# Layer 0 of a four-layer network: attention's first inputs and the mixer's last norm change their stage

## The chip, the cores and the metric

The kernel runs on one core of one Trainium2 chip. A core has a matrix engine (TensorE, PE in the profile; PEld is its weight load), a vector engine (VectorE, DVE), a scalar engine for activations (ScalarE, ACT), a general engine (GpSimd, POOL) and a sync engine that issues DMAs (SyncE, SP). SBUF is the memory the engines work in, 128 partitions wide; PSUM holds what PE produces. The metric is the device time of one execution in microseconds, lower is better.

## What is computed

Input x has the shape (4, 32, 128, 128): batch, time, node, feature. Four layers follow one another; the change touches the first, the three others stay. Layer 0 adds to x, after a group norm over features, the result of an attention over nodes followed by a selective state-space mixer over time:

```python
def _gat(h, adj, Wq, Wk, Wv, Wo, bo):
    q = (h @ Wq).reshape(BT, N, HEADS, HD)      # likewise k, v
    scores = einsum('bnhd,bmhd->bhnm', q, k) / sqrt(HD)
    scores = where(adj == 0, -1e9, scores)
    o = einsum('bhnm,bmhd->bnhd', softmax(scores), v)
    return h + o.reshape(BT, N, D_MODEL) @ Wo + bo

def _mamba(xt, ...):                            # x and z from in_proj, short convolution, silu
    dt = softplus(...); dA = exp(dt[..., None] * A); dBx = (dt * xc)[..., None] * Bm
    def step(hprev, inp):
        hnew = dA_t * hprev + dBx_t
        return hnew, einsum('bds,bs->bd', hnew, C_t)
    ...                                         # 32 steps, 16 states, 256 channels
    return ((ys + Dp * xc) * silu(z)) @ out_w + out_b
```

A layer norm (gain ns_g, ns_b) follows the attention, another (nt_g, nt_b) the mixer together with its own input.

## The kernel before, in words

x lies whole in SBUF as X, nodes on the partitions. `layer0` (L265) loads weights and then goes through the four batches, one after the other: `gat` (L379) is the attention of one batch, `mamba` (L671) its mixer. Each has pools of its own that are opened before and closed after it: l0g in SBUF and l0sc, l0po, l0px in PSUM for attention, l0m, l0m2 in SBUF and l0pa, l0y in PSUM for the mixer. The pools of one stage lie where those of the other lay, so that a tile's first writer waits for the last user of whatever was at its place. l0s (with the state S), l0w and the two PSUM banks pm are open through the whole layer.

**Attention** takes 8 groups of 4 time steps. First, once for a batch, `diags` (L401 to L408) makes three small columns and two diagonal matrices from the group norm's values gd, PE spreads them over the partitions (L412), and ACT copies the result to grow (L416). For a group g: four transposes of X on PE, the normed hg on DVE (L435), q and k on PE (L441) and ACT (L444), v on PE (L450) and DVE (L453), base on POOL (L457, two instructions; it needs grow and X), the scores on PE (L464 masks, L472 products), minima on DVE (L481), exponentials on ACT (L486), sums and reciprocals on DVE (L493, L494), the scaling on POOL (L498), transposes, copies (L506), the products with v (L513), the output projection (L526), residual, norm and the store into h1 (L558). hg, base and xn lie in S, which is free in that stage.

**The mixer** makes 32 steps. In each, four quarters (four states each) run through POOL (L702, the product of dt and A), ACT (L708, exponential), DVE (L722, times the state S) and DVE again (L730, four instructions, or L742 after ACT's L738), and PE reads the state (L755). Every 4 steps there is a block: its preparation (`mamba_block`) and its output, which is projected on PE (L823 to L829), copied by ACT (L835), and normed and added to X: statistics on DVE (L842, L844, L845), a power on POOL (L848), a shift on DVE (L852), the norm on ACT (L857), three instructions on POOL (L861, L862, L864). `gat_head` (L322) computes the group norm's values of the next batch inside the mixer after step 23: transposes, statistics, two small products with g4 (L356) with DVE work between them (L360 to L363), a power on POOL (L369).

**The order** is written by a planner, `Parts`. Every piece of work is a part with an engine, a cost in us, what it comes after, what it takes and frees (`hold`: how many buffers of a name there are), and a rank. `emit` repeatedly picks the earliest startable part by these costs and, within 0.15 us of it on the same engine, the lowest rank; a rank is step times pace plus an offset by kind (GAT_RANKS, PREP_RANKS, RANKS). `in_order` then fixes the order on each of PE, ACT, DVE and POOL for the whole plan. Each attention and each mixer is a plan of its own, so on every engine all of a mixer's instructions stand before all of the next attention's. The head's rank is T * pace with T = 32 and a pace of 25.5.

Of the kernel before, what the change touches and what calls it, by code (L numbers as in the profile page):

```python
# [187 lines left out]
class Kernel:  # L188
# [76 lines left out]
    def layer0(self):  # L265

        with self.pool("l0h", 1) as hp, self.pool("l0c", 1) as c:
            h1 = hp.tile([P, 3 + T, N], F32, tag="h1", name="h1")
            self.nc.gpsimd.memset(h1[:, :3, :], 0.0)


            with self.pool("l0s", 1) as m, self.pool("l0w", 2) as w, self.pool("l0pm", 2, True) as pm:
                S = m.tile([P, T * N], F32, tag="S", name="S")

                for t in range(0, T, 8):
                    self.load_x(0, t, t + 8)
                gw = self.gat_weights(c)
                with self.pool("l0k", 1) as k:
                    mw, built = self.mamba_weights(c, k)
                    for b in range(1, B):  # L280
                        self.load_x(b)
                    plan = Parts()
                    d = self.gat_head(plan, 0, gw, m, pm)
                    with self.in_order():
                        plan.emit()
                    built()
                for b in range(B):
                    with self.pool("l0g", 2) as g, self.pool("l0sc", 2, True) as ps, self.pool("l0po", 1, True) as po:
                        with self.pool("l0px", 1, True) as px:
                            blks = self.gat(b, h1, S, d, gw, mw, g, m, w, ps, po, px, pm)  # L290
                    with self.pool("l0m", 1) as y, self.pool("l0m2", 2) as v:
                        with self.pool("l0pa", 2, True) as pa, self.pool("l0y", 1, True) as py:
                            d = self.mamba(b, h1, S, blks, gw, mw, m, w, y, v, pa, py, pm)

    def gat_weights(self, c):
# [16 lines left out]
        att=-560, back=1038.5, base=200, den=-2290.5, diag=1387, eT=-3745, expo=1373, hg=-1936.5, norm=-205,  # L312
        o=-720.5, power=2945, proj=-444.5, q=-340.5, qo=-606, r=-2536, sc=-4037, scale=6881.5, smin=435,
        stats=4037.5, store=1820, turn=-662, v=3273.5, vo=-1137, x=401,
# [3 lines left out]
        back=-674.5, bc=5118, bct=1491.5, conv=1508, dabs=-687.5, dbc=1712, dexp=648.5, dln=-965, dplus=1619,  # L318
        dsub=2247.5, dtproj=441.5, one=-448.5, relu=-2119, umul=-703, xproj=836.5, xsilu=645, xturn=-1090.5,
    )  # L320

    def gat_head(self, plan, b, gw, c, pm, after=()):  # L322
# [53 lines left out]
        add(POOL, 0.6, power, [p])  # L376
        return d

    def gat(self, b, h1, S, d, gw, mw, w, m, w2, ps, po, px, pm):  # L379
# [3 lines left out]
        isq = 1.0 / math.sqrt(32)  # L383
        plan = Parts(window=250, patience=0.15)
        hold, pace, s = plan.hold, 144.5, {}
# [15 lines left out]
        def diags():  # L401
            c = s["c"] = w.tile([P, 2], F32, tag="gc", name="gc")
            nc.vector.tensor_tensor(c[:, 0:1], d[0][:, 2:3], d[0][:, 2:3], ALU.add)
            nc.vector.scalar_tensor_tensor(c[:, 1:2], d[0][:, 0:1], -1.0, c[:, 0:1], ALU.mult, ALU.mult)
            nc.vector.tensor_tensor(c[:, 1:2], c[:, 1:2], bo, ALU.add)
            s["D"] = w.tile([P, 2, P], F32, tag="gD", name="gD", bufs=1)
            for i in range(2):
                nc.vector.tensor_scalar(s["D"][:, i, :], self.ident, c[:, i : i + 1], None, ALU.mult)  # L408

        def spread():  # L410
            s["p"] = bank()
            nc.tensor.matmul(s["p"][:, :256], self.ones, s["D"].rearrange("p a b -> p (a b)"), start=True, stop=True)  # L412

        def rowed():
            s["row"] = w.tile([P, 2, P], F32, tag="grow", name="grow", bufs=1)
            nc.scalar.copy(s["row"].rearrange("p a b -> p (a b)"), s.pop("p")[:, :256])  # L416

        p = add("diag", 0, DVE, 1.2, diags)
        hp = hold("pm", 2)
        p = add("diag", 0, PE, 0.5, spread, [p], [hp])  # L420
        row = add("diag", 0, ACT, 0.4, rowed, [p], (), [hp])

        def group(g):
            v = {}
            for i, n in enumerate(("hg", "base", "xn")):
                o = 512 * (2 * i + g % 2)
                v[n] = S[:, o : o + 512]
            xs = X[:, b * T + 4 * g : b * T + 4 * g + 4, :]

            def inputs():  # L430
                v["x"] = bank()
                self.transposes(four(v["x"]), [xs[:, i, :] for i in range(4)])

            def scaled():
                nc.vector.tensor_scalar(  # L435
                    v["hg"], v.pop("x"), d[0][:, 0:1], d[0][:, 2:3], ALU.subtract, ALU.mult
                )

            def proj(n):
                v["p" + n] = bank()  # L440
                nc.tensor.matmul(v["p" + n], Wq if n == "q" else Wk, v["hg"], start=True, stop=True)  # L441

            def proj_out(n):
                nc.scalar.mul(new(v, n), v.pop("p" + n), -isq if n == "q" else 1.0)  # L444

            def values():
                v["pv"] = bank(px, "px")
                for i in range(4):
                    cs = slice(i * P, (i + 1) * P)
                    nc.tensor.matmul(v["pv"][:, cs], v["hg"][:, cs], Wv, start=True, stop=True)  # L450

            def values_out():
                nc.vector.tensor_copy(new(v, "v"), v.pop("pv"))  # L453
# [108 lines left out]
            h = {n: hold(n, 2) for n in ("q", "k", "v", "mn", "xn", "hg", "base")} | {n: hold(n, 1) for n in ("o", "r")}  # L562
            hx, hs, ho = hold("px", 1), [hold("ps", 2), hold("ps", 2)], hold("po", 1)
            hp = hold("pm", 2)
            p = add("x", g, PE, 0.5, inputs, (), [h["hg"], hp])
            x = add("hg", g, DVE, 0.6, scaled, [p], (), [hp])
            outs = []
            for n in ("q", "k"):
                hp = hold("pm", 2)
                p = add("q", g, PE, 0.95, lambda n=n: proj(n), [x], [h[n], hp], [h["hg"]])  # L570
                outs.append(add("qo", g, ACT, 0.55, lambda n=n: proj_out(n), [p], (), [hp]))
            pv = add("v", g, PE, 1.0, values, [x], [h["v"], hx], [h["hg"]])
            vo = add("vo", g, DVE, 0.6, values_out, [pv], (), [hx])
# [41 lines left out]
    def mamba_weights(self, c, k):  # L615
# [20 lines left out]
        ob4 = c.tile([1, 4, P], F32, tag="ob4", name="ob4")  # L636
        for i in range(4):
            nc.sync.dma_start(ob4[:, i, :], ins["L0_conv_out_b"].rearrange("(o n) -> o n", o=1))
# [22 lines left out]
    HEAD = 5  # L661
# [9 lines left out]
    def mamba(self, b, h1, S, blks, gw, mw, m0, w0, m, w, pa, py, pm):  # L671
# [15 lines left out]
        S, d = S.rearrange("p (s d) -> p s d", s=16), None  # L687
# [129 lines left out]
        def output(k, g):  # L817
# [15 lines left out]
            def fetch():  # L833
                g["x"] = w.tile([P, 4, P], F32, tag="xn", name="xn")
                nc.scalar.copy(g["x"].rearrange("p a f -> p (a f)"), g.pop("p"))  # L835

            def stats():
                st = w.tile([P, 4, 6], F32, tag="mst", name="mst")
                g["mv"] = w.tile([P, 4, 2], F32, tag="mmv", name="mmv")
                g["rs"] = w.tile([P, 4], F32, tag="mrs", name="mrs")  # L840
                for i in range(4):
                    nc.vector.bn_stats(st[:, i, :], g["x"][:, i, :])  # L842
                for i in range(4):
                    nc.vector.bn_aggr(g["mv"][:, i, :], st[:, i, :])  # L844
                nc.vector.tensor_scalar(g["rs"], g["mv"][:, :, 1], 1e-5, None, ALU.add)  # L845

            def power():
                nc.gpsimd.tensor_tensor(g["rs"], g["rs"], self.mhalf.to_broadcast([P, 4]), ALU.pow)  # L848

            def shift():  # L850
                g["nb"] = w.tile([P, 4], F32, tag="mnb", name="mnb")
                nc.vector.scalar_tensor_tensor(g["nb"], g["mv"][:, :, 0], -1.0, g["rs"], ALU.mult, ALU.mult)  # L852
# [16 lines left out]
            p = add("stats", 4 * k + 4, DVE, 2.0, stats, [p])  # L869
            p = add("power", 4 * k + 4, POOL, 1.0, power, [p])  # L870
            p = add("shift", 4 * k + 4, DVE, 0.2, shift, [p])
            p = add("norm", 4 * k + 4, ACT, 1.8, norm, [p])
            add("sums", 4 * k + 4, POOL, 4.3, sums, [p], free=[hx])


# [4 lines left out]
        for k in range(T // 4):  # L880
# [7 lines left out]
            if b + 1 < B and k == self.HEAD:  # L888
                plan.rank = T * pace
                d = self.gat_head(plan, b + 1, gw, m0, pm, [last["read", 0]])  # L890
        with self.in_order():
            plan.emit()
        return d
# [2257 lines left out]
```

## Time and profile before

| | us |
|---|---|
| median of 3 runs | 3819.91 (3813.42 to 3825.31) |
| the profiled execution | 3815.5 |
| its span in the trace | 3813.6 |
| layer 0 in it | 0 to about 2287 |

| engine | busy us | share of the span |
|---|---|---|
| PE | 3154.9 | 83% |
| DVE | 2963.4 | 78% |
| ACT | 2671.6 | 70% |
| POOL | 2482.6 | 65% |

The windows view gives the busy time of the engines in layer 0's stages:

| stage | us | PE | DVE | ACT | POOL |
|---|---|---|---|---|---|
| batch 0 attention, 32.0 to 160.0 | 128.0 | 111.3 | 86.1 | 87.8 | 70.8 |
| batch 0 mixer, 160.0 to 597.9 | 437.9 | 358.5 | 402.5 | 381.7 | 397.1 |
| batch 3 attention, 1727.7 to 1855.0 | 127.3 | 109.7 | 88.0 | 89.8 | 72.8 |
| batch 3 mixer, 1855.0 to 2287.0 | 432.0 | 362.9 | 392.1 | 379.9 | 394.6 |

A line of the timeline has start, duration, engine, line and operation, output and inputs, the number of instructions merged, and in brackets how long the engine had been idle before it and what ended that. Lines merged over several instructions overlap with lines between them. A group's line has engine, operation, tiles and count, the durations in ns (minimum, median, maximum), the first and last start in us, and the shape. In a wait, the first name is the instruction that waited, the second what it waited for.

### The profile page before, as it was taken

The page shows a single profiled execution, that of the slowest core. Times are in us where ns is not written, and L with a number is a line of the kernel's source. Part 1 is how long each engine was busy: PE and PEld are TensorE (multiplying, and loading weights), DVE is VectorE, ACT ScalarE, POOL GpSimd, SP SyncE. Part 2 cuts the span into 40 slices and gives each one's busy share as a digit, 9 for nine tenths or more (in the row PEclk, how much of TensorE's full clock was granted, in tenths as well). Part 3 has the DMA queues.
Part 4 walks back from the last instruction along what each step waited for, and adds up shares of the span by engine and source line. Part 5 has one row for each costly group of instructions (what it writes and reads, how often), then busy time and mean ns, then how long its engine had stood idle before and what let it go on. Part 6 is the DMA issues. An engine that isn't in the chain of part 4 may idle for free. (4 is left out here: it accounts for less than half of the span.)

```text
span 3813.6 us, 64481 instructions
## 1 busy us (share of the span) xinstructions
PE 3154.9 (83%) x23495; PEld 2067.5 (54%) x23495; DVE 2963.4 (78%) x7050; ACT 2671.6 (70%) x5577; POOL 2482.6 (65%) x1947
## 2 busy tenths in 40 slices
PE   6888877888878888877888878787868987988878
PEld 4545444555445554544555547665546753587655
DVE  5699996799996799996799975577869856386942
ACT  5899975899975899976899963334565654176753
POOL 3699985799985799975799970133456522067940
PEclk8898999899989899989899875797869998998989
DMA  3000000000000000000000000000002000700003
GB/s 127 1 1 1 1 1 1 1 1 1 1 1 1 1 1 1 1 1 1 1 1 1 1 7 12 1 1 1 1 9 90 1 1 1 269 5 1 1 1 89
DMA packets 51660, 61.38 MB, mean 16 GB/s; under 512 B 5853, under 2 KB 31146, under 8 KB 51210
## 3 DMA queue, kind: packets, MB, share of 16 engines
q1 hardware_dynamic: 36746, 42.12, 3.2%
q10 hardware_dynamic: 14592, 15.08, 1.1%
q8 instruction: 188, 3.08, 0.3%
q14 instruction: 134, 1.10, 0.1%
HBM read 48.80 MB, written 8.39 MB: 15 GB/s over the span
## 5 line engine op out<-in xcount | busy, mean ns | idle before, releaser
L702 POOL TENSOR_TENSOR e<-dt,Ar 128x1024 f32<-128x1024 f32 x496 | 1162.1, 2365 | 48.1 <-ACT pa L708 47.4
L722 DVE TENSOR_TENSOR pa<-pa,S 128x1024 f32<-128x1024 f32 x496 | 608.1, 1226 | 37.5 <-ACT pa L708 36.6
L730 DVE SCALAR_TENSOR_TENSOR S<-u,BC,pa 128x256 f32<-128x256 f32 x1488 | 615.3, 476 | 19.4
L708 ACT ACTIVATE pa<-e 128x1024 f32<-128x1024 f32 x496 | 503.2, 1018 | 82.0 <-DVE S L730 45.4
L755 PE MATMUL yp<-S,Dp 64*64 64x256 f32 x4096 | 350.8, 464 | 84.2 <-DVE S L730 46.0
L755 PE MATMUL yp<-S,D 64*64 64x256 f32 x4096 | 311.9, 412 | 55.8 <-DVE S L742 28.9
L755 PEld LDWEIGHTS yp<-S,Dp 64*64 64x64 f32 x4096 | 183.8, 160 | 232.1 <-issue 137.2
L755 PEld LDWEIGHTS yp<-S,D 64*64 64x64 f32 x4096 | 158.0, 140 | 190.7 <-ACT D L714 50.7
L714 ACT ACTIVATE D<-I,BC 128x64 f32<-128x64 f32 x1024 | 259.3, 336 | 2.7 <-PE yp L755 2.7
L944 PE MATMUL pm<-h,Wm 128*128 128x512 f32 x512 | 238.0, 605 | 1.0 <-ACT sz L910 1.0
L738 ACT ACTIVATE ub<-u,BC 128x256 f32<-128x256 f32 x496 | 210.8, 497 | 0.5 <-DVE S L742 0.3
L773 PE MATMUL pm<-I,y 128*128 128x64 f32 x1024 | 158.1, 281 | 50.5 <-ACT y L763 50.5
L498 POOL TENSOR_TENSOR e<-e,den 128x512 f32<-128x512 f32 x128 | 131.1, 1040 | 78.2 <-DVE den L494 36.6
L773 PEld LDWEIGHTS pm<-I,y 128*128 128x128 f32 x1024 | 147.9, 208 | 58.2 <-ACT y L763 58.2
L719 POOL TENSOR_TENSOR Dp<-I,BC 128x256 f32<-128x256 f32 x256 | 156.0, 621 | 31.0 <-PE yp L755 17.9
L742 DVE TENSOR_TENSOR S<-pa,ub 128x1024 f32<-128x1024 f32 x124 | 151.7, 1224 | 5.7
L944 PEld LDWEIGHTS pm<-h,Wm 128*128 128x128 f32 x512 | 91.3, 189 | 111.6 <-issue 98.3
L486 ACT ACTIVATE e<-sc,mn 128x128 f32<-128x128 f32 x512 | 145.5, 393 | 6.0 <-DVE mn L481 5.9
L763 ACT COPY y<-yp 128x512 f32<-128x512 f32 x128 | 73.6, 575 | 82.8 <-PE yp L755 82.8
L768 PE MATMUL pm<-xc,DD 128*128 128x128 f32 x512 | 127.6, 334 | 0.0
L481 DVE TENSOR_REDUCE mn<-sc 128x4 f32<-128x512 f32 x128 | 80.6, 682 | 49.2 <-PE sc L472 49.2
L768 PEld LDWEIGHTS pm<-xc,DD 128*128 128x128 f32 x512 | 84.9, 208 | 61.1 <-issue 53.6
(594 smaller groups left out, 8178.2 us busy)
## 6 DMA issues: line engine op xcount, KB each, us to landing
w<-in_L_ffn_weight_dram SPq DMA_DIRECT2D x22, 1024.0 KB, 14.2
w<-in_L_ffn_weight_dram ACTq DMA_DIRECT2D x10, 1024.0 KB, 13.2
out_dram<-o ACTq DMA_DIRECT2D x16, 256.0 KB, 2.9
out_dram<-o SPq DMA_DIRECT2D x16, 256.0 KB, 2.9
X<-in_x_dram SPq DMA_DIRECT2D x4, 512.0 KB, 4.8
A<-in_L_conv_A_log_dram SPq DMA_DIRECT2D x1, 2048.0 KB, 9.8
cw<-in_L_conv_conv_w_dram SPq DMA_DIRECT2D x1, 512.0 KB, 10.6
sh<-in_sh_dram SPq DMA_DIRECT2D x1, 512.0 KB, 3.9
```

Of the source, the lines that this page charges most:

```text
L702: nc.gpsimd.tensor_tensor(v["e", q], node("dt").unsqueeze(1).to_broadcast([P, 4, 256]), Ar[:, 4 * q : 4 * q + 4, :], ALU.mult)
L708: nc.scalar.activation(v["a", q], v.pop(("e", q)), AF.Exp, scale=-1.0)
L714: nc.scalar.activation(v["D", q][:, r, :], I2, AF.Copy, scale=g["BC"][:, i, s : s + 1])
L719: nc.gpsimd.tensor_tensor(v["D", q], I2.unsqueeze(1).to_broadcast([P, 4, 64]), C, ALU.mult)
L722: nc.vector.tensor_tensor(v["a", q], v["a", q], S[:, 4 * q : 4 * q + 4, :], ALU.mult)
L730: nc.vector.scalar_tensor_tensor(S[:, s, :], node("u"), Bt, a[:, r, :], ALU.mult, ALU.add)
L738: nc.scalar.activation(v["b", q][:, r, :], node("u"), AF.Copy, scale=g["BC"][:, i, s : s + 1])
L742: nc.vector.tensor_tensor(S4, v.pop(("a", q)), v.pop(("b", q)), ALU.add)
L755: nc.tensor.matmul(v["y"][o : o + 64, n, :256], D[ns, r, :], S[ns, s, :], start=(s < 2), stop=(s >= 14), skip_group_check=True,)
L768: nc.tensor.matmul(v["p"][:, j * P : (j + 1) * P], DD[:, j, :], g["xc"][:, j, cs], start=True, stop=False)
L773: nc.tensor.matmul(v["p"][:, o : o + 64], v["y"][:, n, j * P : (j + 1) * P], I2, start=False, stop=(n == 1))
L944: nc.tensor.matmul(g["x", j], Wm[:, i, j * P : (j + 1) * P], rows(4 * k + 3 - i), start=(i == 0), stop=(i == 3))
```

## The change

A new pool l0e, open through the layer and with two buffers of a name, holds attention's hg, q, k, v, gc and grow, and the mixer's xn with its small statistics tiles. hg leaves S; base and xn of attention move down in it. What were the first steps of attention become two methods, `gat_open` (the diagonals, their spread and copy; the diagonals lie in a buffer of hg) and `gat_inputs` (x, hg, q, k, v of one group). The mixer of batches 0 to 2 calls them for the next batch, for groups 0 and 1, after the head, in its own plan; there v goes through pm instead of px, and all these parts have the rank 31 * pace. The head's rank goes from 32 * pace to 27 * pace. The mixer's last block leaves its norm (`close`) to the next attention's plan; in the last batch it stays. In the norm of every block, the addition of 1e-5 and the shift go from DVE to POOL, which now has four small instructions in place of one. GAT_RANKS and PREP_RANKS have new values. In the first attention, which opens itself, the transposes come after grow. out_b is loaded by one DMA in place of four and read with a stride of 0. The descriptor scratch of the program is set to 1024.

```diff
-            with self.pool("l0s", 1) as m, self.pool("l0w", 2) as w, self.pool("l0pm", 2, True) as pm:
+            with (
+                self.pool("l0s", 1) as m, self.pool("l0w", 2) as w, self.pool("l0e", 2) as e,
+                self.pool("l0pm", 2, True) as pm,
+            ):
...
-            d = self.mamba(b, h1, S, blks, gw, mw, m, w, y, v, pa, py, pm)
+            early = self.mamba(b, h1, S, blks, gw, mw, m, w, e, y, v, pa, py, pm)
...
+    def gat_open(self, add, hold, d, after, gw, e, pm):
...
+            c = s["c"] = e.tile([P, 2], F32, tag="gc", name="gc")
...
+            s["D"] = e.tile([P, 512], F32, tag="hg", name="hg")[:, :256].rearrange("p (a b) -> p a b", a=2)
...
+        p = add("diag", 0, DVE, 1.2, diags, after)
+        hp = hold("pm", 2)
+        p = add("diag", 0, PE, 0.5, spread, [p], [hp])
+        s["ready"] = add("diag", 0, ACT, 0.4, rowed, [p], (), [hp])
+        return s
+
+    def gat_inputs(self, add, hold, s, b, g, gw, e, pm, px):
...
+        hp = hold("pm", 2)
+        p = add("x", g, PE, 0.5, inputs, [s["ready"]], [h["hg"], hp])
+        x = add("hg", g, DVE, 0.6, scaled, [p], (), [hp])
+        v["outs"] = []
+        for n in ("q", "k"):
+            hp = hold("pm", 2)
+            p = add("q", g, PE, 0.95, lambda n=n: proj(n), [x], [h[n], hp], [h["hg"]])
+            v["outs"].append(add("qo", g, ACT, 0.55, lambda n=n: proj_out(n), [p], (), [hp]))
+        hx = hold("px", 1) if px else hold("pm", 2)
+        p = add("v", g, PE, 1.0, values, [x], [h["v"], hx], [h["hg"]])
+        v["vo"] = add("vo", g, DVE, 0.6, values_out, [p], (), [hx])
...
+        if early:
+            s = early
+            s["ready"] = None
+            s.pop("close")(lambda kind, at, *args, **kwargs: add("c" + kind, 0, *args, **kwargs))
...
+        else:
+            s = self.gat_open(add, hold, d, (), gw, ew, pm)
...
-            for i, n in enumerate(("hg", "base", "xn")):
+            if g not in s["v"]:
+                self.gat_inputs(add, hold, s, b, g, gw, ew, pm, px)
+            v = s["v"][g]
+            for i, n in enumerate(("base", "xn")):
...
-                nc.vector.tensor_scalar(g["rs"], g["mv"][:, :, 1], 1e-5, None, ALU.add)

             def power():
+                g["nb"] = e0.tile([P, 4], F32, tag="mnb", name="mnb")
+                nc.gpsimd.tensor_scalar(g["rs"], g["mv"][:, :, 1], 1e-5, None, ALU.add)
+                nc.gpsimd.tensor_scalar(g["nb"], g["mv"][:, :, 0], -1.0, None, ALU.mult)
                 nc.gpsimd.tensor_tensor(g["rs"], g["rs"], self.mhalf.to_broadcast([P, 4]), ALU.pow)
-
-            def shift():
-                g["nb"] = w.tile([P, 4], F32, tag="mnb", name="mnb")
-                nc.vector.scalar_tensor_tensor(g["nb"], g["mv"][:, :, 0], -1.0, g["rs"], ALU.mult, ALU.mult)
+                nc.gpsimd.tensor_tensor(g["nb"], g["nb"], g["rs"], ALU.mult)
...
+            if early and k == T // 4 - 1:
+                early["close"] = lambda add: close(add, None, [])
+            else:
+                close(add, p, [hx])
...
-                plan.rank = T * pace
-                d = self.gat_head(plan, b + 1, gw, m0, pm, [last["read", 0]])
+                plan.rank = self.HEADED * pace
+                d, p = self.gat_head(plan, b + 1, gw, m0, pm, [last["read", 0]])
+
+                def ahead(kind, at, *args, **kwargs):
+                    plan.rank = self.EARLIER * pace + at
+                    return plan.add(*args, **kwargs)
+
+                early = self.gat_open(ahead, hold, d, [p], gw, e0, pm)
+                for g in range(self.EARLY):
+                    self.gat_inputs(ahead, hold, early, b + 1, g, gw, e0, pm, None)
```

## The prediction

> **What bounds the kernel now.** I read the windows view first, cut at the stage boundaries of layer 0. Four times an attention stage is followed by a mixer stage, so the trace has three places where a mixer ends and the next attention begins. Each holds a hole some 25 us long. The columns are length, then busy us (instructions) of PE, PEld, DVE, ACT, POOL, the granted clock, DMA:
>
> ```profile
> 1711.50:1736.80 25.30, 15.19 (x105) 9.21 (x106) 5.64 (x29) 6.25 (x13) 9.61 (x8) 0.80 0.00 1
> 581.00:606.50 25.50, 14.66 (x100) 8.79 (x100) 6.42 (x29) 6.25 (x13) 9.61 (x8) 0.80 0.00 0
> 1147.70:1173.00 25.30, 14.56 (x92) 8.73 (x96) 6.23 (x29) 6.25 (x13) 9.62 (x8) 0.80 0.00 1
> ```
>
> DVE works about 6 of 25 us, ACT 6, POOL 10: the holes are waiting, not work. The timeline of the third shows the order:
>
> ```profile
> 1710.27 1.22 DVE L742 TENSOR_TENSOR S<-pa,ub 128x1024 f32<-128x1024 f32 x1
> ...
> 1718.27 0.39 PE L829 MATMUL pm<-ident,h 128*128 128x128 f32 x2
> ...
> 1726.46 1.26 POOL L864 TENSOR_TENSOR X<-X,xn 128x512 f32<-128x512 f32 x1
> 1727.75 0.16 DVE L403 TENSOR_TENSOR gc<-gd 128x1 f32<-128x1 f32 x1 [5.79 <-POOL X L864]
> ...
> 1728.61 1.52 DVE L435 TENSOR_SCALAR S<-pm,gd 128x512 f32<-128x512 f32 x2
> ...
> 1734.60 1.03 PE L464 MATMUL sc<-far,identb 128*128 128x512 bf16 x4
> 1735.55 0.98 PEld L472 LDWEIGHTS sc<-k,q 32*128 32x128 f32 x32 [0.42 <-issue]
> 1735.56 1.17 PE L472 MATMUL sc<-k,q 32*128 32x128 f32 x32
> ...
> 1736.76 2.48 DVE L481 TENSOR_REDUCE mn<-sc 128x4 f32<-128x512 f32 x4 [6.63 <-PE sc L472]
> ```
>
> The last scan step ends at 1711.49 (L742), the mixer's last projection on PE at 1718.66 (L829). The last norm then crosses ACT, DVE, POOL, ACT, POOL until 1727.72 (L864), and only then does attention's first DVE instruction start (L403): its small tile lies where the mixer's xn lay. After it come hg, q, k, and at 1736.76 the first softmax minimum. Attention thus starts 18.1 us after PE is done with the mixer.
>
> Inside the mixer DVE is the engine that is rarely idle: from 1655.0 to 1711.5 it is busy 53.45 of 56.50 us, against 43.53 for POOL and 38.76 for ACT. By line (ns are minimum/median/maximum), three lines that touch only SBUF vary widely there, and two that read PSUM do not:
>
> ```profile
> L845 DVE TENSOR_SCALAR mrs<-mmv x32: 170/2056/2201, 231.1 to 2279.3; 128x4 f32<-128x4 f32 x32
> L852 DVE SCALAR_TENSOR_TENSOR mnb<-mmv,mrs x32: 161/502/1715, 236.1 to 2280.6; 128x4 f32<-128x4 f32 x32
> L363 DVE TENSOR_TENSOR gd<-gd,gmv x4: 159/2193/2193, 17.2 to 1651.3; 128x1 f32<-128x1 f32 x4
> L435 DVE TENSOR_SCALAR S<-pm,gd x32: 781/803/810, 33.0 to 1804.1; 128x512 f32<-128x512 f32 x32
> L453 DVE COPY v<-px x32: 658/670/692, 43.2 to 1824.7; 128x512 f32<-128x512 f32 x32
> ```
>
> Four elements per partition take 0.17 us when POOL is idle and 2.06 in the median: they end when POOL's 2.36 us product (L702) ends.
>
> **The change, part by part.** The profiled execution took 3815.5 us (span 3813.6, 1.9 around it); it lies 4.4 under the median 3819.91. I sum against 3815.5.
>
> A. *Hole.* Groups 0 and 1 have hg, q, k and v in their own pool before the mixer ends, and attention's first buffers no longer wait for the last norm. What is late next is the projection on PE, since every plan keeps each engine in order: scores can start at 1718.7, and L464 to the end of L472 took 1734.60 to 1736.73, 2.13 us. First minimum at 1720.85 instead of 1736.76: 15.9 us. The norm's statistics, now first on DVE in attention, wait for ACT's copy at 1719.3 and take 1.4 us to 1720.7, still in time. 3 x -15.9 = **-47.7**.
>
> B. *Attention after the first minimum.* It loses two v groups on PE (1.05 + 1.16) and DVE (0.68 + 0.66), one diagonal product (0.4 PE, 0.4 ACT), and gains 1.24 DVE, 1.65 ACT and 1.8 + 3.9 POOL of the moved norm. POOL is busy 73 of 127 us there and hides its part. I take -1 each, **-3**; ends -5 (all of the PE and DVE work shortens it) and +4 (the norm's DVE and ACT work delay the first groups).
>
> C. *Early inputs in three mixers.* They become ready after POOL's power, near 1655 to 1668, where DVE has no slack, so DVE's time counts in full: hg 2 x 0.80, v 2 x 0.67 = 2.94, read from PSUM and so unmoved by POOL. The five small instructions of the diagonals take 1.04 beside an idle POOL (L403 0.16, L404 0.16, L405 0.16, L408 0.48 for two). Beside a busy one no row shows them; the nearest are L361 to L363, the same kind in the same place: 1.73, 0.16, 2.19. So 5, and 8 in all. Low end 4 (quiet rows). High end 20: each of the five waits out a 2.36 us product (11.8), and PE, whose diagonal product stands ahead of the scan's reads in its order, waits as it did for L363 (5.5). PE's 7 us and ACT's 2.8 us of this work stay beside DVE, as these were busy 41.66 and 38.76 of 56.5. 3 x 8 = **+24** (12 to 60).
>
> The Trainium skill, "SBUF — State Buffer", section "Who interferes with whom", speaks against this part: VectorE and GpSimd share a port pair as an exclusive lock, taken by tensor_scalar in its two-port modes and by anything with two SBUF inputs. By the rule all five may be held, an estimate of 12 us instead of 5, which would make C +44 and the time 3787; L362, 0.16 between two held ones, says that not every one is.
>
> D. *Norm off DVE.* L845 and L852 were 44.8 and 15.9 us of DVE over the mixers; both go, for three short POOL instructions that cost 0.79 more than L848 alone (start to start 1.78 at L541 to L544, against 0.99). DVE wins 2.4 per block of 4 steps, but POOL is idle only some 2.5 us of 55 there (53.2 busy of 56.0 between 886 and 942), and becomes the bound. The most is 2.5 - 0.8 = 1.7 per block; I take half, 0.9. With 6 such blocks in 4 mixers: **-22**. Ends: -41 (all of 1.7) and +25 (32 blocks, POOL the bound throughout).
>
> E. *First attention.* Its first DVE instruction waited 3.72 us for ACT's L654, whose tile lay under it; the new pool lies elsewhere, so it can follow Wm at 28.5 instead of 32.19. Against that the transposes now stand behind the diagonal product on PE (0.4 + 0.6) and hg behind them. Three DMA issues fewer on SP (0.3 each) bring the loads behind them 0.9 earlier. **-2** (-4 to +2).
>
> F. *New ranks* reorder attention and the mixer's first block; the head's rank falls from 32 to 27 steps. No row shows the new order. PE is busy 110 of 127 us in an attention, so the gain has an end: 17 each; for the loss I take the same size. Value **0**, the order that the trace has. The smaller descriptor scratch is used by no queue here (no DMA is issued by POOL): 0. The last mixer's tail: POOL's four instructions against POOL then DVE, +0.2: 0.
>
> Sum: -47.7 - 3 + 24 - 22 - 2 = -50.7, so 3764.8 by the profiled execution, 3769.2 by the median. I say **3767**.
>
> **Rivals.**
> 1. *Fuller gain.* The diagonals fall where POOL is idle (C = 12) and DVE's relief is used whole (D = -41): -47.7 - 3 + 12 - 41 - 2 = -82, 3736. For it: POOL waited 11.9 us for ACT's pa in one mixer (L702), which waits for DVE. Against it: POOL has little room.
> 2. *The hole moves into the mixer.* Early work at its dear end for three mixers, +45, and no net gain in D: -47.7 - 3 + 45 - 2 = -8, 3810. For it: DVE's 53.45 of 56.50. Against: only five instructions can be held.
> 3. *Slower: in-order queues behind held DVE work.* The planner prices the diagonals at 1.2 us; on the chip they could take 12. PE's spread, x, q and k are placed by the planner's time, ahead of the scan's reads, and whoever needs those reads (y copy, next step's sums on DVE) waits too. At 5.5 us (L356 behind L363) for each of spread and two groups, C is 3 x (14.7 + 16.5) = 94: -47.7 - 3 + 94 - 22 - 2 = +19, 3837. It decides from (47.7 + 3 + 22 + 2) / 3 = 25 us per mixer on.
> The change not doing what it says would show the first minimum still behind L864: within 5 of no change; it is counted with rival 2.
>
> **Numbers.** Forecast (3745 to 3797) 0.57; rival 1 (3715 to 3745) 0.20; rival 2 (3797 to 3831) 0.15; rival 3 0.08. About 0.3% (11.5 us) is what a measurement here can tell from no change. Faster by more: 0.57 + 0.20 + 0.08 of rival 2 (below 3808) = 0.85; same 0.07; slower 0.08. The range 3725 to 3812 leaves out a third of rival 1 (0.06), the upper part of rival 2 (0.06) and rival 3 (0.08).
>
> **What would show it.** A: the first L481 of attention 2 to 4 within 3 us of the last projection, no wait on L864. C: the early diagonals' mean duration in the mixer, and DVE's busy time after them. D: the pace of a middle block under 55 us, POOL's idle time gone. E: the first attention's first minimum before 40.77. I am wrong if scores wait for something that I don't see behind the projection, if the early instructions stall PE, or if the new ranks move an attention by more than 5 us.

## The result, and the profile after

The changed kernel takes 3863.84 us in the median of 4 runs (3858.76 to 3872.33), beside 3822.61 (3813.42 to 3826.67) for the kernel before: 1.0113 times as long, 95% interval 1.0087 to 1.014. I had said 3767, with 3725 to 3812 as the range and 0.08 for slower. Its profiled execution took 3864.56, with a span of 3862.7 and a mean granted clock of 0.867 (before 0.886).

The windows view of the changed kernel at the three boundaries, from the last scan step to the first minimum (columns as in the prediction):

```profile
1753.10:1763.60 10.50, 10.50 (x94) 8.02 (x95) 1.49 (x9) 1.17 (x2) 0.00 (x0) 0.84 0.01 2
602.30:611.30 9.00, 8.89 (x95) 6.80 (x96) 1.57 (x11) 1.17 (x2) 0.73 (x1) 1.00 0.01 2
1176.30:1185.40 9.10, 8.86 (x94) 6.77 (x95) 1.67 (x10) 1.17 (x2) 0.00 (x0) 1.00 0.01 2
```

The hole of 25 us is 9 to 10.5 long, and PE is busy throughout: the boundary is now work of PE. The timeline of the third:

```profile
1751.80 1.22 DVE L784 TENSOR_TENSOR S<-pa,ub 128x1024 f32<-128x1024 f32 x1
...
1754.52 1.49 PE L517 MATMUL sc<-far,identb 128*128 128x512 bf16 x3
...
1761.49 0.39 PE L871 MATMUL pm<-ident,h 128*128 128x128 f32 x2
...
1762.02 1.17 PE L525 MATMUL sc<-k,q 32*128 32x128 f32 x32
...
1762.53 0.87 DVE L884 BATCH_NORM_STATS2 mst<-xn 128x6 f32<-128x128 f32 x4 [4.12 <-ACT xn L877]
...
1763.60 0.66 DVE L534 TENSOR_REDUCE mn<-sc 128x4 f32<-128x512 f32 x1
```

Scores follow the last projection at once (L525 after L871) and the first minimum comes 1.7 us after it, where it was 18.1. Three of attention's four masks (L517) even run on PE before the mixer's end: that all of a mixer's instructions stand before all of the next attention's is so in the kernel before and no longer in the changed one.

Of the three DVE lines that varied beside POOL, the two of the norm are now POOL's (L890 to L893, the last one below), and five early diagonal instructions are new on DVE. The lines of the first three in the changed kernel (ns, minimum/median/maximum; of each four, one is the first attention's, beside an idle POOL, and takes 159):

```profile
L893 POOL TENSOR_TENSOR mnb<-mnb,mrs x32: 202/203/204, 237.3 to 2327.7; 128x4 f32<-128x4 f32 x32
L390 DVE TENSOR_TENSOR gc<-gd x4: 159/2308/2345, 19.7 to 1690.8; 128x1 f32<-128x1 f32 x4
L391 DVE SCALAR_TENSOR_TENSOR gc<-gd,gc x4: 159/1193/1197, 19.9 to 1693.2; 128x1 f32<-128x1 f32 x4
L392 DVE TENSOR_TENSOR gc<-gc,bo x4: 159/159/159, 20.1 to 1694.4; 128x1 f32<-128x1 f32 x4
```

So the aim was reached, and the loss is elsewhere. I cut both traces at four marks in each batch: attention's first minimum, its last store into h1, the mixer's first product (L722, now L764) and its last, and the last projection.

| us | before, batches 0 to 3 | after | sum of differences |
|---|---|---|---|
| start to first minimum | 40.77 | 36.32 | -4.5 |
| last projection to next first minimum | 18.04, 18.10, 18.11 | 1.73, 1.72, 1.72 | -49.1 |
| first minimum to last store | 121.04, 118.12, 118.07, 118.02 | 121.99, 119.87, 119.98, 121.56 | +8.2 |
| last store to first product | 6.12 in each | 11.36, 11.41, 11.40, 11.36 | +21.0 |
| first to last product | 412.62, 415.81, 412.46, 407.82 | 431.42, 432.68, 434.97, 419.00 | +69.4 |
| tails and layers 1 to 3 | | | +4.1 |

The sum is +49.1, the difference of the spans. Two rows carry the loss: a delay at each mixer's start, and the mixers themselves. The last mixer holds no early work and still is 11.2 longer. Three suspicions came from this, in this order: the new places of base and xn in S; the norm's move to POOL, by its operations or by the order that the planner makes of its new parts; and the places of the mixer's tiles, since POOL's product (L702, now L744) takes 2.41 us in the mean where it took 2.365.

**The delay at the start.** In step 0 the mixer fills S with 16 DVE instructions (L732, now L774). The timeline of the kernel before, batch 3, DVE and POOL:

```profile
1851.42 7.74 DVE L732 TENSOR_SCALAR S<-u,BC 128x256 f32<-128x256 f32 x13
1852.91 2.50 POOL L719 TENSOR_TENSOR Dp<-I,BC 128x256 f32<-128x256 f32 x4 [1.81 <-issue]
```

And of the changed one:

```profile
1883.29 2.42 POOL L761 TENSOR_TENSOR Dp<-I,BC 128x256 f32<-128x256 f32 x4 [1.82 <-issue]
1884.16 12.44 DVE L774 TENSOR_SCALAR S<-u,BC 128x256 f32<-128x256 f32 x9 [1.00 <-PE pm L257]
1885.67 2.43 POOL L744 TENSOR_TENSOR e<-dt,Ar 128x1024 f32<-128x1024 f32 x1
1888.06 1.27 POOL L761 TENSOR_TENSOR Dp<-I,BC 128x256 f32<-128x256 f32 x2
1889.30 9.52 POOL L744 TENSOR_TENSOR e<-dt,Ar 128x1024 f32<-128x1024 f32 x4
```

Alone such an instruction takes 0.35 us. Once POOL works, one DVE instruction ends with each POOL instruction: nine from 1884.16 to 1896.59, beside three Dp, a product, two Dp and three products. Before, nine of the 16 were through when POOL began at 1852.91 or just after, and the other seven met one product only. Now base and xn lie in slices of S that step 0 fills early, so that it waits for attention's last transposes of xn (L257): seven of the 16 are through when POOL begins, and of the other nine four meet a product, three more than before.

### The profile page after: what moved, and what is told of

The parts are those of the page before. It is cut to its first block, busy times and chain, and to the rows that moved or that the text cites. A ratio compares the mean times of both kernels' runs of the same rounds, so it can differ in the third digit from the quotient of the medians.

```text
span 3862.7 us, 64454 instructions
## 1 busy us (share of the span) xinstructions
PE 3226.3 (84%) x23495; PEld 2133.5 (55%) x23495; DVE 2948.8 (76%) x6986; ACT 2683.8 (69%) x5577; POOL 2523.8 (65%) x2043
## 5 line engine op out<-in xcount | busy, mean ns | idle before, releaser
L744 POOL TENSOR_TENSOR e<-dt,Ar 128x1024 f32<-128x1024 f32 x496 | 1180.5, 2411 | 40.9 <-ACT pa L750 40.1
L764 DVE TENSOR_TENSOR pa<-pa,S 128x1024 f32<-128x1024 f32 x496 | 607.8, 1225 | 97.0 <-ACT pa L750 95.8
L797 PE MATMUL yp<-S,D 64*64 64x256 f32 x4096 | 346.1, 431 | 119.4 <-DVE S L784 63.9
L797 PEld LDWEIGHTS yp<-S,D 64*64 64x64 f32 x4096 | 180.1, 147 | 251.5 <-DVE S L784 61.2
L998 PE MATMUL pm<-h,Wm 128*128 128x512 f32 x512 | 241.1, 616 | 1.0 <-ACT sz L964 1.0
L815 PE MATMUL pm<-I,y 128*128 128x64 f32 x1024 | 168.9, 294 | 45.5 <-ACT y L805 45.5
L815 PEld LDWEIGHTS pm<-I,y 128*128 128x128 f32 x1024 | 158.5, 221 | 54.7 <-ACT y L805 54.6
L998 PEld LDWEIGHTS pm<-h,Wm 128*128 128x128 f32 x512 | 94.8, 195 | 117.1 <-issue 107.6
L2795 ACT ACTIVATE xn<-X,xnb,xrs 128x128 f32<-128x128 f32 x192 | 80.7, 487 | 42.8 <-DMA lnw<-in_L_attn_ln_w_dram 30.6
```

The lines of the kernel that those rows point to most:

```text
L744: nc.gpsimd.tensor_tensor(v["e", q], node("dt").unsqueeze(1).to_broadcast([P, 4, 256]), Ar[:, 4 * q : 4 * q + 4, :], ALU.mult)
L764: nc.vector.tensor_tensor(v["a", q], v["a", q], S[:, 4 * q : 4 * q + 4, :], ALU.mult)
L797: nc.tensor.matmul(v["y"][o : o + 64, n, :256], D[ns, r, :], S[ns, s, :], start=(s < 2), stop=(s >= 14), skip_group_check=True,)
L815: nc.tensor.matmul(v["p"][:, o : o + 64], v["y"][:, n, j * P : (j + 1) * P], I2, start=False, stop=(n == 1))
L998: nc.tensor.matmul(g["x", j], Wm[:, i, j * P : (j + 1) * P], rows(4 * k + 3 - i), start=(i == 0), stop=(i == 3))
```

## The experiments

Each was run in several rounds against the kernel before, whose median was 3817 to 3824; a ratio is to that.

**1. base and xn back to their old columns**

```diff
-                o = 512 * (2 * i + g % 2)
+                o = 512 * (2 * (i + 1) + g % 2)
```

> The changed kernel with attention's base and xn back at their former places in S (xn in the state slices 8 to 11, not 4 to 7). Theory 1 (the 21 us between attention's last store and the first product of the mixer come from step 0: its DVE writes of slices 4 to 7 now wait for the last attention transposes, fall behind POOL's start, and are then let through one per POOL instruction): the stretch from the last store to the first product goes from 11.4 to 6.1 us in each batch, the whole from 3864 to about 3843, the mixers unchanged. Rival (the new order of attention's end sets it): 11.4 stays, 3864.

3834.92 us, ratio 1.0035 (1.0019 to 1.0051), 29 under the changed kernel. The last store to the first product is 6.12 in all four batches, so the place in S is the cause of that delay. Of the 29, the starts are 21; in the profiled executions the attentions are 4.3 shorter as well and the mixers 2.9. The mixers stay long (433.5, 431.0, 430.3, 420.4).

**2. The changed kernel with the norm's small operations on DVE again, in the old parts**

```diff
-                p = add("power", 4 * k + 4, POOL, 1.3, power, [p])
+                p = add("power", 4 * k + 4, POOL, 1.0, power, [p])
+                p = add("shift", 4 * k + 4, DVE, 0.2, shift, [p])
...
-                nc.gpsimd.tensor_scalar(g["rs"], g["mv"][:, :, 1], 1e-5, None, ALU.add)
+                nc.vector.tensor_scalar(g["rs"], g["mv"][:, :, 1], 1e-5, None, ALU.add)
...
-                nc.gpsimd.tensor_tensor(g["nb"], g["nb"], g["rs"], ALU.mult)
+                nc.vector.scalar_tensor_tensor(g["nb"], g["mv"][:, :, 0], -1.0, g["rs"], ALU.mult, ALU.mult)
```

> The changed kernel with the norm's small operations back on DVE and planned as before. Theory 2 (the norm on POOL makes the mixers 11 us longer each, because POOL is the bound and because ACT's norm waits for four POOL instructions at the head of its queue): the last mixer, which has no early work, goes from 419 back to about 408 from first to last product, the whole from 3864 to about 3820. Rival (something else in the new kernel, such as where its buffers lie, slows POOL's products from 2.36 to 2.41 us and the mixers with them): the last mixer stays at 415 to 419, the products at 2.41, the whole within 15 of 3864, or above it by what DVE pays again.

3826.50, ratio 1.0 (0.9981 to 1.0019); mixers 420.9, 423.8, 423.4, 410.9. (The shift of a mixer's last block also gets a rank in attention's plan, here and in experiments 5, 7, 9 and 11.) Undoing the move gains 37. That seemed to condemn the operations on POOL, but the edit takes back two things at once, the operations and the parts that the planner sees. The next two part them, in the kernel before.

**3. The kernel before with the norm's small operations on POOL, in the new part** (operations as in the change)

```diff
-            p = add("power", 4 * k + 4, POOL, 1.0, power, [p])
-            p = add("shift", 4 * k + 4, DVE, 0.2, shift, [p])
+            p = add("power", 4 * k + 4, POOL, 1.3, power, [p])
```

> The kernel before with one part of the change alone: the norm's small operations on POOL, planned as the change plans them (1.3 on POOL, no shift). Theory 2: each mixer 9 to 13 us longer, the whole at about 3865. Rival (the loss is in the buffers' places or in the early work): at or below 3822, by the prediction's term D some 3800.

3867.73, ratio 1.0119 (1.0093 to 1.0146); mixers 430.3, 428.4, 430.5, 415.2. This one part of the change has the changed mixers' loss.

**4. The same operations, the planner told the old parts**

```diff
-            p = add("shift", 4 * k + 4, DVE, 0.2, shift, [p])
+            p = add("shift", 4 * k + 4, DVE, 0.2, lambda: None, [p])
```

> As the run before, but the planner is told of the old parts (1.0 on POOL and a shift of 0.2 that issues nothing), so that every other instruction keeps its old order. If the operations themselves cost the time (POOL as the bound): about as slow as the run before. If the reordering that the new costs bring is what costs: at or below 3822, as DVE is rid of 61 us; by term D about 3800.

3794.81, ratio 0.9933 (0.9912 to 0.9954); mixers 408.4, 405.9, 405.9, 398.3. The instructions are those of experiment 3; only their order differs, and it is worth 73 us. In the old order the operations on POOL gain 29.

**5. The changed kernel with both edits** (columns of 1, planner told the parts of 4)

> The changed kernel with two edits: base and xn at their former places in S, and the planner told of the norm's old parts (1.0 on POOL, a shift of 0.2 that issues nothing). Theory 2b (what the norm's move cost was the new order its parts brought, not its operations): the mixers lose what the first pair of runs differed by, some 18 each, so the last mixer from 420 to about 402, the whole from 3835 to about 3765, and faster than both kernels. Rival (with early work in the plan the order is another anyway): the last mixer near 400 to 405, as it has no early work, but the first three stay near 430, the whole at 3815 or above.

3760.40, ratio 0.9851 (0.9822 to 0.9879), faster than both kernels: boundaries 1.72, starts 6.12, mixers 409.8, 409.9, 413.4, 406.7.

**6. Experiment 4 with one number changed**

```diff
-            p = add("power", 4 * k + 4, POOL, 1.0, power, [p])
+            p = add("power", 4 * k + 4, POOL, 1.3, power, [p])
```

> The kernel before with the norm's small operations on POOL and the old parts (3795), but the one number 1.0 for POOL's part replaced by 1.3, which is nearer to what it takes (1.78). If the lost part (the shift on DVE, which holds the norm back) made the bad order: 3795 to 3805. If any new cost makes a worse order, as the ranks fit one set of costs: 3820 to 3870.

3854.10, ratio 1.009 (1.0068 to 1.0113): 59 more for 0.3 us of a cost estimate.

**7. Experiment 5 without early inputs** (the diagonals stay in the mixer; hg, q, k and v of groups 0 and 1 go to attention)

```diff
-    HEAD, HEADED, EARLIER, EARLY = 5, 27, 31, 2
+    HEAD, HEADED, EARLIER, EARLY = 5, 27, 31, 0
```

> As the first of this set, but with no group's inputs in the mixer (the diagonals and grow stay there). By the prediction's terms A and C: the wait between the last projection and the first minimum grows from 1.7 to about 9 us, as x, hg, q and k of group 0 come back into it, and the mixer's part from step 24 to 28 gets 3 to 6 us shorter in each of the first three batches; the whole +5 to +15 over the first of this set. Rival (the early inputs stall the mixer by more than they save): faster than the first of this set.

3770.28, ratio 0.9877 (0.9854 to 0.99). The boundary is 7.56 in place of 1.72, 17.5 over three, of which the mixers give back some: early inputs are worth about 10. All four runs were slower than those of experiment 5, but the intervals of the two ratios overlap, so the size isn't sure.

**8. Experiment 4 with 16 KB of unused SBUF ahead of the mixer's pools, one row of out_b and the smaller scratch**

```diff
+                pad = e.tile([P, 4096], F32, tag="pad", name="pad")
+                self.nc.gpsimd.memset(pad[:, :1], 0.0)
...
+        ob = self.load(c, "ob", ins["L0_conv_out_b"].rearrange("(o n) -> o n", o=1), [1, P])
+        ob4 = ob.unsqueeze(1).to_broadcast([1, 4, P])
...
-    nc = bacc.Bacc("TRN2", target_bir_lowering=False, num_devices=1)
+    nc = bacc.Bacc("TRN2", target_bir_lowering=False, num_devices=1, dynamic_dma_scratch_size=1024)
```

> The kernel before with the norm's operations on POOL and the old parts (3795), and an unused buffer of 16 KB where the change puts its pool, the single row of out_b and the smaller descriptor scratch: the same instructions in the same order at other places in SBUF. Theory 3 (POOL's products take 2.41 instead of 2.36 us because of where dt, e and Ar lie): products at 2.40 or more, 0 to 23 us slower than 3795. Rival (they are slowed by what runs beside them): products stay at 2.367, 3795.

3795.10, ratio 0.9937 (0.9915 to 0.9959), POOL's product at 2.37 us. None of the three costs anything that shows.

**9. The changed kernel, planner told the old parts, nothing else**

```diff
-                p = add("power", 4 * k + 4, POOL, 1.3, power, [p])
+                p = add("power", 4 * k + 4, POOL, 1.0, power, [p])
+                p = add("shift", 4 * k + 4, DVE, 0.2, lambda: None, [p])
```

> The changed kernel with its own layout of S, but with the planner told the old two parts of the norm (power 1.0 on POOL, an empty shift 0.2 on DVE). Theory: the order that came from the new parts costs what it cost between the layout run (3834.9) and the run with both edits (3760.4), 74 us, whether or not the layout is mended: 3864 - 74 = 3790 (3780 to 3800), with 11.4 us between attention's last store and the first product of each mixer as in the changed kernel, and mixers of 405 to 415 us. Rival: the two edits help one another, and without the mended layout the old order is not worth that much: 3820 or more.

3779.31, ratio 0.9881 (0.9845 to 0.9917): 84.5 under the changed kernel, 11 more than I expected. Mixers 411.0, 410.6, 411.2, 405.4. The starts are 11.54, 6.13, 11.55, 11.55; the second is short because POOL there stands 1.94 us for PE before its next Dp (717.17), and step 0's last writes are through by 717.22 beside a single product. To experiment 5 it is 19, the price of the columns, of which the three long starts are 16.

**10. The kernel before, one number changed** (every instruction stays, but for four table loads of ACT that the new order spares)

```diff
-            p = add("power", 4 * k + 4, POOL, 1.0, power, [p])
+            p = add("power", 4 * k + 4, POOL, 1.3, power, [p])
```

> The kernel before, with one number changed: the planner prices power at 1.3 instead of 1.0. Every instruction is the one it was, with the same tiles; only the order on the engines differs, and it is the order of the run that had this number with the norm's operations on POOL. Theory: the order alone makes it slower, by what that number cost there (3794.8 to 3854.1, +59): 3822 + 59 = 3882 (3860 to 3900), mixers about 14 us longer each. Rival: the order is only bad with the norm's operations on POOL, which then has too much to do: 3810 to 3835, mixers 405 to 418.

3883.54, ratio 1.0174 (1.0151 to 1.0198): +61, by the order alone. The windows view of its last mixer, and below it that of the kernel before:

```profile
1912.39:2334.43 422.04, 358.25 (x2846) 214.01 (x2842) 383.01 (x652) 370.30 (x682) 378.90 (x219) 0.87 0.00 1
```

```profile
1860.90:2268.72 407.82, 348.14 (x2846) 205.05 (x2842) 383.24 (x652) 369.11 (x683) 379.12 (x219) 0.89 0.00 1
```

DVE, ACT and POOL do the same work to within 1.2 us, and the stage is 14.2 longer: they lose the time in waits. PE is busy 10.1 longer with the same instructions, at a granted clock of 0.87 in place of 0.89. A lower clock goes with longer runs in one order too (the 33 runs of the kernel before beside these experiments go from some 3811 us at 0.892 to 3839 at 0.877), but it doesn't make up the difference: at the same clock of 0.879, experiment 4 took 3794.81 and 3798.92 and experiment 6, whose order is the one here, 3851.24. Step 19 of this mixer (counted from 0) takes 21.4 us where it took 15.7; its timeline, POOL, ACT and DVE:

```profile
2154.02 6.99 POOL L702 TENSOR_TENSOR e<-dt,Ar 128x1024 f32<-128x1024 f32 x3
...
2166.45 1.28 ACT L992 ACT_TABLE_LOAD   x1 [0.18 <-DVE dt L983]
...
2167.74 1.06 ACT L992 ACTIVATE u<-u 128x1024 f32<-128x1024 f32 x1
...
2168.88 2.36 POOL L998 TENSOR_TENSOR dt<-dt,u 128x1024 f32<-128x1024 f32 x1 [7.87 <-ACT u L992]
...
2170.10 2.98 ACT L714 ACTIVATE D<-I,BC 128x64 f32<-128x64 f32 x12
...
2173.09 1.28 ACT L910 ACT_TABLE_LOAD   x1
...
2175.36 0.59 ACT L763 COPY y<-yp 128x512 f32<-128x512 f32 x1
...
2176.92 1.28 ACT L708 ACT_TABLE_LOAD   x1
2177.37 0.42 DVE L781 TENSOR_TENSOR yg<-pm,sz 128x256 f32<-128x256 f32 x1 [4.90 <-PE pm L773]
...
2179.34 1.23 DVE L722 TENSOR_TENSOR pa<-pa,S 128x1024 f32<-128x1024 f32 x1 [0.77 <-ACT pa L708]
```

POOL has no products left at 2161.0 and stands 7.87 us for the next block's dt, which waits for ACT's logarithm (L992). ACT then has diagonals, the gates' silu and two table loads ahead of its next exponential (L708 at 2178.28), and DVE stands 4.90 for PE, which needs ACT's copy of y (L763) from behind the silu. Both engines that set the pace are idle in turn, because the block's logarithm stands four exponentials, a whole step, later in ACT's order. In the kernel before, POOL went from a product to the same L998 without a wait:

```profile
2094.45 2.35 POOL L702 TENSOR_TENSOR e<-dt,Ar 128x1024 f32<-128x1024 f32 x1 [0.52 <-ACT pa L708]
...
2095.69 1.06 ACT L992 ACTIVATE u<-u 128x1024 f32<-128x1024 f32 x1
...
2096.82 2.36 POOL L998 TENSOR_TENSOR dt<-dt,u 128x1024 f32<-128x1024 f32 x1
```

The logarithm is late in this way in all four batches: steps 16 to 19 take 61.2, 61.6, 63.1 and 61.7 us where they took 52.0, 52.8, 52.0 and 55.6. That is 35 of the 63 us that the four mixers lose; the rest I did not follow. Over the layer the groups of the kernel before and of this one say the same of L998 (busy us, mean ns, idle before it):

```profile
L998 POOL TENSOR_TENSOR dt<-dt,u 128x1024 f32<-128x1024 f32 x32 | 75.5, 2358 | 13.3 <-ACT u L992 13.1
```

```profile
L998 POOL TENSOR_TENSOR dt<-dt,u 128x1024 f32<-128x1024 f32 x32 | 75.3, 2354 | 54.1 <-ACT u L992 53.9
```

In the changed kernel the same wait (its L1052) is 30.5, DVE's for PE before yg 57.9 (before 18.7), and DVE's for the exponential 95.8 (before 36.6): another order, with a loss of the same kind.

**11. Experiment 5 with 64 more unused bytes in the new pool**

```diff
+                pad = e.tile([P, 16], F32, tag="pad", name="pad", bufs=1)
+                self.nc.gpsimd.memset(pad[:, :1], 0.0)
```

> The run with both edits and 64 more bytes per partition ahead of the early buffers, which nothing uses. In the program POOL's product e lies at byte 207360 of a partition in the kernel before and at 212416 in the changed one: a multiple of 128 and one that is 64 off. With the pad it is at 212480, again a multiple of 128. Theory: that is why the product took 2.43 us in the changed kernel and its variants and 2.37 in the kernel before and its variants. Then the mean falls to 2.37, POOL has 124 x 0.06 = 7.6 us less in each mixer, the mixers come to 400 to 406 and the time to 3730 to 3745. Rival: something else in the changed program slows the product; then it stays at 2.42 to 2.43 and the time at 3755 to 3770.

3749.65, ratio 0.9821 (0.98 to 0.9842), the fastest version here. The product's durations, experiment 5 and then this one:

```profile
L744 POOL TENSOR_TENSOR e<-dt,Ar x496: 2377/2424/2569, 158.9 to 2204.2; 128x1024 f32<-128x1024 f32 x166
```

```profile
L746 POOL TENSOR_TENSOR e<-dt,Ar x496: 2340/2363/2424, 156.9 to 2182.1; 128x1024 f32<-128x1024 f32 x166
```

The product is as quick as in the kernel before. The time fell by 11, less than the 15 to 30 I expected, and the two ratios' intervals overlap: the duration is sure, the size of the gain isn't. Mixers 408.6, 411.6, 408.1, 395.6; in the last POOL is busy 381.8 of 395.6 us.

**12. Experiment 4 with e 64 bytes off** (a pool of its own, behind l0w)

```diff
+                pad = e.tile([P, 16], F32, tag="pad", name="pad")
+                self.nc.gpsimd.memset(pad[:, :1], 0.0)
```

> The run with the norm on POOL in the old order (3794.8, product 2.37 us) and 64 unused bytes per partition ahead of the mixer's own tiles, so that e lies 64 off a multiple of 128 (207424), as in the changed kernel. Nothing else moves. Theory: the product takes 2.41 to 2.43 us, and the time is 3808 to 3825. Rival: the place doesn't matter: 2.36 to 2.37 us and 3790 to 3800.

3792.17, ratio 0.9927 (0.9908 to 0.9947), the product 2.37 in the mean. So a place 64 bytes off a multiple of 128 isn't slow by itself. With 11, the place of some tile decides, and the rule isn't found.

## Why the prediction was wrong, point by point

- **A, the hole: right.** -15.9 each, measured -16.4. What is late next is the projection on PE, as said.
- **E, first attention:** -2, measured -4.5, just past my end of -4; the sign is right, the path isn't. The diagonals start at 19.71, before Wm and not behind it, and then the first minimum stood 6.87 us for ACT's Ar (L696, in the kernel before L654), a wait for the same instruction that I had counted as gone.
- **C, early inputs: the five instructions right in size, the whole smaller.** The early diagonals in the third mixer took 2.30, 1.20, 0.16 and 1.50 for two, 5.15 us against my 5. The Trainium skill ("SBUF — State Buffer", "Who interferes with whom") says that an instruction that needs the shared ports is blocked for the whole of the other's; by it I had estimated 12. L392, with two inputs in SBUF, took 0.16 in the mixers too, between held ones. That doesn't speak against the page: in all three mixers it starts in the 0.07 us between two POOL instructions (1694.38 in the third, between 1694.33 and 1694.41), as L362 did in the kernel before. All six short ones seen beside a busy POOL found such a gap. PE and ACT are a little late behind them: DVE then stood 0.87 for the one and 2.21 for the other. As a whole, experiment 11's first three mixers beside experiment 4's are 8 us longer in sum, or 16 if the last one's -2.7 is taken as the effect of all else. I had 24, with 12 as the low end.
- **D, the norm off DVE: right in the old order.** -22, measured -29 (experiment 4), and -47, past my end of -41, between experiments 2 and 9, which share one order; 5 of these are experiment 9's short start. POOL became the busiest engine, as I said: in experiment 4's last mixer 382.4 of 398.3 us, DVE 369.5 (before 379.1 and 383.2 of 407.8).
- **B, attention:** -3, measured +8.2, outside my ends. In experiment 11 the four come to +0.7, so most of it isn't the moved norm itself. An attention also takes some 118 or 121 us with no change of its own: in experiments 4, 8 and 12 its order is that of the kernel before, and two or three of the four take 121, where one did. I did not part it further.
- **F, the order: the step that failed.** I put new orders at 0, with a loss of up to 17 in an attention for the ranks, of which nothing went into the range, and thought of attention and a mixer's first block only; in D I counted instructions in the order of the old trace. But the change gives the planner one part of 1.3 in place of 1.0 and 0.2, and that re-orders the mixers' blocks. Experiments 3 against 4 show 73 us for it, 9 against the changed kernel 84.5, and 10 shows 61 with no operation changed. The new ranks, which I did name, were not tested by themselves; they are in experiment 11 as well, whose last mixer takes 395.6 beside 398.3 in experiment 4, so that no loss of theirs shows there.
- **Not priced: the places in S.** I had read that DVE is held by POOL, and the diff moves base and xn, but I did not ask what step 0 waits for. +21 in the traces; in the whole time experiment 1 shows 29 for it, and experiment 9 against 5 shows 19.
- **Rivals.** The third had the right side and the wrong mechanism: it blames the early work, but the last mixer has none and lost 11.2, and experiment 10 has none anywhere.

From the changed kernel down, the loss is 84.5 (order), 19 (places in S) and 11 (places of tiles, the least sure), and what is left is 72.5 under the kernel before, beside the 50.7 that I had summed.

## What to carry to other kernels

Where a planner writes the order, a changed cost or a merged part is a change of every later placement. Price it as unknown on both sides, with the size that orders have shown, and on the chip take the operations apart from the order first, by giving the planner the old parts. A truer cost doesn't make a better order: POOL's four instructions take 1.78 us, so 1.3 was nearer than 1.0, and it was 59 us slower.

When tiles change place under a buffer that two stages share, follow which slice the next stage writes first, and who still reads it then.

## What I had not expected of the hardware

- Beside a busy POOL, a DVE instruction that works from SBUF to SBUF (L774) got through once for each POOL instruction, whatever its length: 0.35 us alone, 0.46 to 0.70 beside Dp, 2.43 to 2.47 beside a product (batch 3 of the changed kernel). A delay of two instructions at the wrong moment cost 5.2 us.
- The same POOL product took 2.37 us or 2.43 in programs that differ by 64 unused bytes. Which tile's place matters stays open.
- In the profiled executions the granted clock was lower in the slow orders (0.867 to 0.877, against 0.881 to 0.892 in the others and before), and PE's reads of the state took 451 ns in the changed kernel against 438 before. Over all runs the two overlap (0.867 to 0.879 and 0.877 to 0.894). Most of the loss stands at an equal clock (experiment 10); whether the clock adds the rest or only follows from the waits stays open.
